# New durations, half clock and exclusion in a kernel's own list scheduler: two transformer blocks on one core

## The chip, the core and the metric

The kernel runs on one core of a Trainium2 chip. A core has five engines with a queue of instructions each: PE (TensorE, matmuls; its weight loads are listed as PEld), DVE (VectorE), ACT (ScalarE), POOL (GpSimd) and SP (SyncE, which here issues all DMAs). An engine takes its instructions strictly in the order of its queue and waits at each for semaphores of other engines. The metric is the device time of one execution in microseconds (us); lower is better. [...]

## The reference

Two blocks on x of shape (16, 512, 256), float32; every block has layer norm, a scale and shift per batch row, a token mixer, a gated residual, and the same again with a feed-forward part:

```python
h = _layernorm(x) * (1 + ca) + sa
x = x + ga * _L0_attn_ref(h, ...)      # fast weights: a recurrence over chunks of 16 tokens
h = _layernorm(x) * (1 + cb) + sb
x = x + gb * _L0_ffn_ref(h, ...)       # low rank, gelu
...
x = x + ga * _L1_attn_ref(h, ...)      # attention over a window of 64 tokens, 4 global tokens
x = x + gb * _L1_ffn_ref(h, ...)       # mix of a token with the one before, sigmoid * relu^2
```

The recurrence of the first block, per chunk and head, with two small weight matrices `W_in` and `W_out`:

```python
k_h = softmax(k_t . W_in) * lr;  q_h = softmax(q_t . W_in)
o_t = q_h . W_out + tril(q_h k_h^T) v_t
W_out = W_out + k_h^T v_t
for _ in range(2):
    g_out = -attn(W_in, k_t, v_t);  g_in = -attn(W_out, v_t, k_t)
    W_in = W_in - lr_in * g_in;     W_out = W_out - lr_out * g_out
```

## The kernel before

The work is cut into 16 units: 2 halves of the batch (8 rows each) times 8 blocks of 64 tokens. A unit `u` passes five streams:

- `prepare`: layer norm, projections to q, k, v (matmuls `pp`, L712), a short convolution on DVE (L731, three multiply-adds on `pp`), Silu on ACT, and spills of the results to DRAM (L740).
- `chain`: the recurrence. A unit has two pieces of 32 tokens, a piece two chunks of 16. `load_piece` brings a piece back (`dt_k`, `dt_v`, `dt_q`, L838) and scales it: ACT's square, DVE's reduction `ss_k`, `ss_q` (L850), Pool's product (L852). `recur` does a chunk. Its larger steps: scores of tokens and weights on DVE (L798 a product of 128x1024, L799 its sum), exponentials on ACT (L813), scalings on DVE (L820, L894), outer products on POOL (L805: `pd_o`, `pd_kv`, `pd_i`), their sums on DVE (L907). `pd_kv` is turned into running sums by an addition (L899), a scan (L902) and a copy (L903), all on DVE; POOL then makes the output of it (L932 to L934). `finish_piece` normalizes the output and stores it (L953).
- `mlp`: output projection (`pwo`, L979), residual, low-rank feed-forward (`ph`, `pQ`).
- `attend`: windowed attention. Per row group `r` of four: scores `sc` and their maxima (`mx`, L1160 on DVE, then with the global tokens' L1171, then copies on POOL, L486 and L488), scores again transposed (`st`), exponentials, `py` and `pz`, and the quotient `yT` on DVE (L1252, after `rs` on ACT, L1247 and L1248). The layer norm in front of it ends in `off_c` (L624), `xn_c` (L630), PE transposes and the scalings `hTc` (L638).
- `mix`: the second feed-forward part. `mixture` (L1301 on ACT, L1302 on DVE) blends a token with the one before.

The chains of the two halves run beside each other, and the streams of several units overlap: the program is written in the order of a coarse table of times (`timetable`). That order isn't the one that runs. When all instructions have been recorded, the class `Timetable` orders each engine's queue anew:

- `read` makes a `Step` of every instruction and finds from the tiles' cells which steps must come after which.
- `Step.cost` gives each step a duration: how long its engine is busy, and when its result is there.
- `run` is a list scheduler. Again and again it takes, over all engines, the step that can start first (ties: the first in program order), puts it at the end of its engine's queue, and marks when the engine is free and when the result is there. A step starts when its engine is free (`idle`), what it waits for has ended (`since`, with a `HOP` from engine to engine) and a buffer of its ring is free (`room`). On ACT, `table` keeps functions of another table in bursts.
- `pin` fixes the resulting order for every engine, and which tile follows which in a buffer.

So the durations set the order of all queues, PE's, DVE's, ACT's, POOL's and SP's, and nothing else of the program. Where DVE, ACT or POOL follow each other on the engine, the scheduler lets the next one start `EARLY` (83, 105 or 45 ns) before the result of the last.

## Time and profile before

| what | value |
|---|---|
| three runs | 3047.35, 3049.54, 3053.68 us (median 3049.54) |
| the profiled execution | 3055.67 us, of which 3053.9 us are the span from the first to the last instruction |
| mean granted clock of TensorE | 0.805 of full speed |
| DMA | 186.41 MB in 439304 packets, mean 61 GB/s |
| largest groups on POOL | L805 pd_i 303.6 us, pd_o 301.2, pd_kv 179.4; L932 156.3 |
| largest groups on DVE | L902 206.1 us, L1160 163.7, L798 sc_k 155.4, L907 di 154.2 |
| largest groups on PE | L1144 st 217.1 us, sc 201.9; L1274 pproj 129.0 |

A page of a profile gives the busy time of each engine, the span in 40 slices (each digit the busy share in tenths; PEclk the clock that TensorE was granted), the chain of work that ended last, and the costliest groups of instructions: line, engine, operation, result<-operands, count, then busy time and mean duration of one in ns, then the idle time of the engine in front of them and what ended it. A timeline row has start, duration, engine, line, operation. A matmul of float32 operands stands in the records as two.

### The profile page before, as it was taken

The numbers are of one execution on the slowest core, as the hardware profiler recorded it, in microseconds if no ns is written. First come the engines' busy times: TensorE is split into PE (matmuls) and PEld (weight loads), VectorE is DVE, ScalarE is ACT, GpSimd is POOL, SyncE is SP. The second block draws the span as 40 slices with busy tenths as digits, with TensorE's granted clock in tenths as the row PEclk, the third lists the DMA queues.
The fourth block names the chain that finished last, engine by engine and source line by source line (L and its number), as shares of the span: only waits on it lengthen the run. The fifth ranks groups of instructions, "written<-read, shape, count | busy, mean of one in ns | idle before, by whom it ended". The sixth has DMA issues, their size and how long they took to land.

```text
span 3053.9 us, 46422 instructions
## 1 busy us (share of the span) xinstructions
PE 2271.9 (74%) x16784; PEld 1407.7 (46%) x16784; DVE 2407.6 (79%) x4513; ACT 1705.7 (56%) x3805; POOL 1646.7 (54%) x1447
## 2 busy tenths in 40 slices
PE   3640156788878785887879788887978887898996
PEld 2210124454535354453545455463555555565664
DVE  1689889889898989879797988979697987975321
ACT  1771354575656565565656556575655645454553
POOL 0246656557565576656465565645556565654212
PEclk7775576888878796878879787888978787888998
DMA  5430113132305041230504123140413312122010
GB/s 158 100 68 7 49 35 75 36 81 53 88 22 119 21 102 39 61 80 22 117 24 105 36 68 73 35 106 22 116 25 75 67 53 60 39 63 60 22 29 28
DMA packets 439304, 186.41 MB, mean 61 GB/s; under 512 B 323937, under 2 KB 413090, under 8 KB 439074
## 3 DMA queue, kind: packets, MB, share of 16 engines
q1 hardware_dynamic: 439074, 183.44, 25.0%
q8 instruction: 132, 2.16, 0.3%
q14 instruction: 98, 0.80, 0.1%
HBM read 116.66 MB, written 66.72 MB: 60 GB/s over the span
## 4 chain that ended last, share of the span: by engine, by line
DVE 48%; PE 25%; ACT 11%; POOL 6%; issue 5%; DMA 3%; SPq 1%; POOLq 0%; DVEq 0%; ACTq 0%
DVE pd_kv L902 5%; PE st L1144 4%; DVE sc_v L798 4%; DVE sv L799 4%; DVE scs L799 3%; DVE sc_k L798 3%; DVE di L907 2%; DVE do L907 2%; DVE mx L1160 2%; DVE mix L1302 2%; PE pwo L979 2%; POOL pd_kv L805 2%; DVE pp L731 2%; PE sc L1144 2%; DVE sc_q L798 2%
## 5 line engine op out<-in xcount | busy, mean ns | idle before, releaser
L805 POOL TENSOR_TENSOR pd_o<-e_k,dt_v 128x1024 f32<-128x1024 f32 x128 | 301.2, 2361 | 273.6 <-DVE e_k L820 273.5
L805 POOL TENSOR_TENSOR pd_i<-e_v,dt_k 128x1024 f32<-128x1024 f32 x128 | 303.6, 2400 | 66.8 <-DVE e_v L820 66.8
L1144 PE MATMUL sc<-keys,qs 32*128 32x128 f32 x2048 | 201.9, 307 | 91.7 <-DVE yT L1252 61.1
L1144 PE MATMUL st<-qs,keys 32*128 32x128 f32 x2048 | 217.1, 339 | 68.5 <-DVE mx L1160 56.3
L1144 PEld LDWEIGHTS st<-qs,keys 32*128 32x128 f32 x2048 | 189.1, 233 | 108.1 <-DVE mx L1160 54.7
L1144 PEld LDWEIGHTS sc<-keys,qs 32*128 32x128 f32 x2048 | 164.9, 203 | 155.3 <-DVE yT L1252 65.7
L902 DVE TENSOR_TENSOR_SCAN pd_kv<-within,pd_kv 128x1024 f32<-128x1024 bf16 x64 | 206.1, 3220 | 0.7
L979 PE MATMUL pwo<-w_WoT,oT 128*128 128x256 f32 x256 | 95.9, 528 | 133.7 <-POOL oT L972 133.7
L932 POOL TENSOR_TENSOR pd_kv<-hid,pd_kv 128x1024 f32<-128x1024 f32 x64 | 156.3, 2442 | 60.3 <-DVE fw L903 58.9
L805 POOL TENSOR_TENSOR pd_kv<-hid,dt_v 128x1024 f32<-128x1024 f32 x64 | 179.4, 2803 | 17.0 <-DVE hid L894 17.0
L1160 DVE TENSOR_REDUCE mx<-sc 128x4 f32<-128x512 f32 x256 | 163.7, 676 | 26.1 <-PE sc L1141 25.7
L907 DVE TENSOR_REDUCE di<-pd_i 128x64 f32<-128x1024 f32 x128 | 154.2, 1210 | 29.5 <-POOL pd_i L805 29.4
L1196 ACT ACTIVATE pT<-st 128x512 f32<-128x512 f32 x256 | 133.5, 603 | 62.4 <-PE st L1141 62.4
L907 DVE TENSOR_REDUCE do<-pd_o 128x64 f32<-128x1024 f32 x126 | 151.8, 1205 | 12.3 <-POOL pd_o L805 12.1
L798 DVE TENSOR_TENSOR sc_k<-tok,fw 128x1024 f32<-128x1024 f32 x128 | 155.4, 1214 | 6.1 <-ACT tok L868 4.6
L798 DVE TENSOR_TENSOR sc_v<-tok,fw 128x1024 f32<-128x1024 f32 x128 | 151.4, 1216 | 1.8
L799 DVE TENSOR_REDUCE sv<-sc_v 128x64 f32<-128x1024 f32 x128 | 151.1, 1209 | 0.0
L1007 PE MATMUL ph<-PT,w_v 64*128 64x512 f32 x256 | 112.1, 800 | 39.6 <-ACT rs L1247 21.7
L1274 PE MATMUL pproj<-w_proj,yT 128*128 128x256 f32 x512 | 129.0, 404 | 15.2 <-ACT sg L495 8.3
L979 PEld LDWEIGHTS pwo<-w_WoT,oT 128*128 128x128 f32 x256 | 65.6, 273 | 150.5 <-POOL oT L972 135.7
L725 ACT COPY xp<-pp 128x512 f32<-128x512 f32 x96 | 56.9, 593 | 138.9 <-PE pp L712 131.7
L1252 DVE TENSOR_TENSOR yT<-py,rs 128x256 f32<-128x256 f32 x128 | 49.4, 415 | 104.3 <-ACT rs L1248 104.3
(244 smaller groups left out, 6605.4 us busy)
## 6 DMA issues: line engine op xcount, KB each, us to landing
values<-values SPq DMA_DIRECT2D x56, 256.0 KB
gate_a<-gates SPq DMA_DIRECT2D x64, 128.0 KB
xa<-in_x_dram SPq DMA_DIRECT2D x32, 256.0 KB
x<-in_x_dram SPq DMA_DIRECT2D x32, 256.0 KB
gate_c<-gates SPq DMA_DIRECT2D x64, 128.0 KB
gate_d<-gates SPq DMA_DIRECT2D x64, 128.0 KB
q<-y SPq DMA_DIRECT2D x64, 128.0 KB
dt_q<-q SPq DMA_DIRECT2D x32, 256.0 KB
```

Of the source, the lines that this page charges most:

```text
L798: engine.tensor_tensor(pr, tok.unsqueeze(1).to_broadcast(every), w.unsqueeze(2).to_broadcast(every), mul)
L799: nc.vector.tensor_reduce(dst, pr, AX.X, add)
L805: engine.tensor_tensor(pr, hid.unsqueeze(2).to_broadcast(every), tok.unsqueeze(1).to_broadcast(every), mul)
L902: nc.vector.tensor_tensor_scan(flat, within, flat, 0.0, mul, add)
L907: nc.vector.tensor_reduce(t, pr, AX.X, add)
L932: nc.gpsimd.tensor_tensor(po, qh.unsqueeze(2).to_broadcast([P, R, D, CH]), upto, mul)
L979: nc.tensor.matmul(po[:, n * C : (n + 1) * C], lhsT=pair(oT, k, 2 * b2 + n), rhs=w_o[:, k, :], start=k == 0, stop=k == 1,)
L1007: nc.tensor.matmul(ph, lhsT=w_v1[rows, f // 2, :], rhs=pT[rows], start=True, stop=True)
L1144: nc.tensor.matmul(dst, lhsT=lhsT, rhs=rhs, start=start, stop=False, skip_group_check=True)
L1160: nc.vector.tensor_reduce(mx[:, j], sc[j].rearrange("p (s k) -> p s k", s=NS), AX.X, ALU.max)
L1196: nc.scalar.activation(pT[j], st[j], AF.Exp)
L1274: nc.tensor.matmul(po[:, n * C : (n + 1) * C], lhsT=yT[:, k2, par].rearrange("p e t -> p (e t)"), rhs=w_proj[:, k2, par, :], start=k2 == 0 ...
```

## The change

The `Step` costs and the scheduler's loop change; all that computes stays. What is new:

```diff
-        self.busy, self.done = self.cost()
+        self.busy, self.rest = self.cost()
...
+        pair = [x for x in ins.ins if hasattr(x, "ap") and free(x) and x.bass_ap.space == bass.MemoryType.SB]
+        self.shares = len(pair) > 1
...
             if ins.is_transpose:
-                return 166, 273
+                return 2 * n / CLOCK, 165
             if str(w.dtype).endswith("bfloat16"):
-                return max(0.52 * n, 110), 0.52 * n + 115
-            rows, cols = list(w.ap)[0][1], size(w)
-            if min(rows, cols) <= 32 and n <= 256:
-                return (62, 275) if max(rows, cols) <= 32 else (0.38 * n + 55, 0.8 * n + 175)
-            return max(1.77 * n, 220), 1.75 * n + 150
+                own, wide = n / CLOCK, 1
+            else:
+                own, wide = max(4 * n / CLOCK, 140), P // max(32, list(w.ap)[0][1]) * (P // max(32, size(w)))
+            wide = min(wide, 4)
+            return own / wide, own - own / wide + (165 if wide == 1 else 65)
         if self.engine == "SP":
-            return 560, 3060
+            far = max(int(np.prod([n for _, n in list(x.ap)])) for x in aps)
+            return (600, LAND + 1300) if far > 2**16 else (530, LAND)
...
         elif self.kind == "InstTensorScalarPtr" and n == R * D * CH:
-            t = 190 + 2.1 * n
+            t = 2285
         else:
-            t = 150 + (1.65 if apart and self.kind == "InstTensorReduce" else 1.04) * n
-        return t - EARLY[self.engine], t
+            t = (150 if n > 64 else 165) + (1.65 if apart and self.kind == "InstTensorReduce" else 1.04) * n
+            t += 60 * (self.kind == "InstTensorScalarPtr")
+        return t - EARLY[self.engine], EARLY[self.engine]
...
                     t = max(t, idle[e], since[k])
+                    if e == "DVE" and steps[k].shares:
+                        t = max(t, pool)
+                    elif e == "Pool":
+                        t = max(t, lock)
...
-            idle[e] = t + s.busy + (TABLE if first else 0)
-            end[k] = t + s.done + (TABLE if first else 0)
+            busy = s.busy + (TABLE if first else 0)
+            if e == "PE":
+                while t >= edge:
+                    warm = used > (BUSY if warm else 0.97) * WINDOW
+                    edge, used = edge + WINDOW, 0.0
+                busy *= 1 if warm else 2
+                used += busy
+            idle[e] = t + busy
+            end[k] = t + busy + s.rest
+            if e == "Pool" and s.shares:
+                pool = end[k]
+            elif e == "DVE" and s.shares:
+                lock = end[k]
```

The constants are `CLOCK, WINDOW, BUSY = 2.4, 3413, 0.6` and `LAND = 2500`. All of the computation stands 22 lines further down in the changed kernel (L902 becomes L924).

More of the change, by code (lines that the diff above doesn't have):

```diff
@@ L104 @@
 TABLE = 1283
+CLOCK, WINDOW, BUSY = 2.4, 3413, 0.6
+LAND = 2500
 OTHER_TABLES = ("Silu", "Tanh", "Gelu_apprx_tanh")
@@ L130, in cost @@
             if ins.is_transpose:
-                return 166, 273
+                return 2 * n / CLOCK, 165
             if str(w.dtype).endswith("bfloat16"):
-                return max(0.52 * n, 110), 0.52 * n + 115
-            rows, cols = list(w.ap)[0][1], size(w)
-            if min(rows, cols) <= 32 and n <= 256:
-                return (62, 275) if max(rows, cols) <= 32 else (0.38 * n + 55, 0.8 * n + 175)
-            return max(1.77 * n, 220), 1.75 * n + 150
+                own, wide = n / CLOCK, 1
[3 more added lines that the diff above has]
+            return own / wide, own - own / wide + (165 if wide == 1 else 65)
         if self.engine == "SP":
-            return 560, 3060
+            far = max(int(np.prod([n for _, n in list(x.ap)])) for x in aps)
+            return (600, LAND + 1300) if far > 2**16 else (530, LAND)
         if self.kind == "InstLoadActFuncSet":
-            return TABLE, TABLE
+            return TABLE, 0
         if self.engine == "Activation":
@@ L280, in run @@
         self.owner, self.lines = {}, {e: [] for e in ENGINES}
-        held = None
+        held, pool, lock = None, 0.0, 0.0
+        warm, edge, used = False, WINDOW, 0.0
         def room(k):
```

## The prediction

> **What bounds the kernel now.** I read the page from the top, then one period of it in time.

> ```profile
> span 3053.9 us, 46422 instructions
> PE 2271.9 (74%) x16784; PEld 1407.7 (46%) x16784; DVE 2407.6 (79%) x4513; ACT 1705.7 (56%) x3805; POOL 1646.7 (54%) x1447
> DVE  1689889889898989879797988979697987975321
> PEclk7775576888878796878879787888978787888998
> DVE 48%; PE 25%; ACT 11%; POOL 6%; issue 5%; DMA 3%; SPq 1%; POOLq 0%; DVEq 0%; ACTq 0%
> ```

> DVE is busiest (79%) and holds 48% of the chain that ended last; PE holds 25%. In the slices DVE stands at 7 to 9 tenths but for the head and the last three slices, where PE has the work alone. The second view is the spread of three DVE operations with two SBUF tensors each: smallest, median and largest duration.

> ```profile
> L902 DVE TENSOR_TENSOR_SCAN pd_kv<-within,pd_kv x64: 2277/3220/4505, 137.0 to 2762.6; 128x1024 f32<-128x1024 bf16 x64
> L1302 DVE SCALAR_TENSOR_TENSOR mix<-hp,c_mu,mix x64: 700/752/2907, 673.7 to 3034.4; 128x512 f32<-128x512 f32 x64
> L1171 DVE TENSOR_TENSOR mx<-mx,mg x48: 165/187/2026, 1152.5 to 2990.2; 128x16 f32<-128x16 f32 x48
> ```

> One shape, and durations that differ by 2 us and more. The timeline says why:

> ```profile
> 1772.80 4.11 DVE L902 TENSOR_TENSOR_SCAN pd_kv<-within,pd_kv 128x1024 f32<-128x1024 bf16 x1
> 1772.42 2.34 POOL L805 TENSOR_TENSOR pd_o<-e_k,dt_v 128x1024 f32<-128x1024 f32 x1
> 1774.71 4.35 POOL L805 TENSOR_TENSOR pd_kv<-hid,dt_v 128x1024 f32<-128x1024 f32 x1
> ```

> The scan waits until Pool's pd_o is through (1774.76) and then runs its 2.2 us, to 1776.91; Pool's next product was issued at 1774.71 and stands still in its turn, 4.35 us instead of 2.34. So the two exclude each other, and a DVE operation that waits goes ahead of Pool's next one. What is lost so on DVE: scans 206.1 us busy less 64 x 2.277 = 60; mix 64 x 1.424 (the group's mean) less 64 x 0.752 = 43; mx 48 x 0.676 less 48 x 0.187 = 23. Together 126 us, 4% of the span.

> From 362 to 2572 us the scans come in groups of four, one unit of work each, 13 intervals of 146 to 180 us; five intervals in the middle are 175 us to within 0.5 and repeat each other. One of them in slices (columns: length, then busy time of PE, PE's loads, DVE, ACT, POOL, granted clock, DMA), its DVE waits, and three rows of the DMA queue:

> ```profile
> 1772.80:1797.80 25.00, 23.24 (x78) 11.88 (x77) 23.77 (x34) 12.77 (x24) 20.74 (x13) 0.87 0.06 18
> 1822.80:1847.80 25.00, 25.00 (x198) 15.36 (x196) 12.21 (x25) 21.07 (x50) 8.01 (x9) 0.85 0.46 110
> 1872.80:1897.80 25.00, 19.97 (x209) 14.72 (x209) 24.01 (x47) 15.01 (x35) 21.64 (x18) 0.62 0.27 54
> ...
> DVE pp L731 <- ACT pp L728: 8.4, 2, 7.9
> DVE ss_q L850 <- ACT sq_q L829: 5.9, 1, 5.9
> DVE yT L1252 <- ACT rs L1248: 4.3, 3, 3.6
> ...
> 1841.16 1.71 SPq L953 DMA_DIRECT2D o<-dt_q  x2
> 1845.03 2.40 SPq L740 DMA_DIRECT2D k<-y  x4
> 1847.48 1.12 SPq L838 DMA_DIRECT2D dt_q<-q  x2
> ```

> Most of a period belongs to DVE, but one stretch belongs to PE: there PE is busy 25.00 of 25 us, DVE 12.21. DVE's waits in a period come to some 24 us, 19 of them in and just behind that stretch. Exclusion costs it another 9.5 us (two scans 1.8 and 1.7, two mix 1.5 and 2.1, two mx 1.3 and 1.1). A period is thus about 140 us of DVE work, 10 of exclusion and 24 of waiting.

> **The change part by part.** No instruction is added, removed or resized. The hand-written scheduler gets other durations, a model of PE's half clock and of the exclusion, and so each engine's queue has another order. I set the queues of the two built programs beside each other (line numbers of before). DVE work is summed with the median durations of the trace.

> *Mix (L1302).* Before, the first pair of a unit stands straight behind the e_v scaling (L820) that lets Pool start its last two of four pd_i (10.11 us in one run at 1904.78), and stalls there twice, 1.5 and 2.1 us. After, it stands behind the third pd_i's reduction (1.2 us) and a score reduction (1.2 us), that is 2.4 us after the third pd_i ended, when the fourth, 2.34 us long, is just through; Pool's next is a cast that waits for a later DVE step. Of the 43 us I take 38 away. Bounds: 43 if all dodge, 0 if DVE comes a little early. Mix is 7 us of work later; behind it wait pka's matmuls and ACT's Relu, whose Pool square keeps its place in Pool's queue, so that I charge nothing; without this slack it is 7 us in each of 13 periods.

> *mx (L1171).* Some move behind a reduction, some only onto the next Pool product. Of 23 us, 6 are taken; bounds 20 and -10.

> *Scans (L902).* Before, 0.27 us of work stand between the addition L899 and the scan; in 1 of 64 it is 2 us or more. After it is 2.2 us on average, in 29 of 64 2 us or more; in a steady period 2.8, 0.2, 1.2 and 8.6. This is less than it seems. The scan of the first half has two Pool products behind its own, pd_o and the other half's pd_kv, ending 2.34 and 4.68 us later. A scan issued 3.1 us later (0.26 + 2.8) has missed the first boundary and waits 1.6 us for the second; before, it waited 1.8 us for the first. The scheduler has Pool's next instruction ready 45 ns before the last one's end and so always sends Pool first, which the chip did not do above. I take 0; bounds -25 and +25 (half of the 60 either way is more than the rows allow).

> *PE's stretch.* The new prices fit the rows better: two 512-column matmuls are 1.71 us apart from the next two (pq at 1842.86, pk at 1844.57), 0.855 each, against 0.853 now and 0.906 before; sixteen 32-column ones took 1.08 us in all, against 0.85 now and 1.66 before. In the queues the reductions mx of a window's last row group (L1160) move forward by 23 us of DVE work (from 83.0 to 60.2 after a period's first scan), off_c (L624), which PE's transposes wait for, by 3 us, and ACT's second rs moves ahead of the hTc scalings, which is what yT waited 3.6 us for. But pp's matmul of the key weights stays behind the same scores and masks. I take 2 of the 13 us off yT's and pp's waits, 13 times: 26. Bounds 0 and 75 (half of the longest of each, 3.6 and 7.9, 13 times).

> *The DMA queue and the second half.* The store of the second o (L953) moves behind the first two spills k<-y (L740). Before, both stores were issued by 1842.9 and the first spill at 1845.03, at 0.6 each; so this store comes some 3.9 us later, and behind it the load dt_q, ACT's square, DVE's ss_q, which is waited for already. ss_q itself also moves behind two mx reductions (1.3 us). I charge 1.5 us in each of 13 periods, 20 in all; bounds 0 and 51. The second half's pd_i reduction is 8.3 us of work later in the period. The load dt_k behind it was issued at 1808.3 and its square ran at 1841, 33 us on, so that I charge nothing; without that slack it is 13 x 8.3 = 108.

> [...] The row is the granted clock, 0.805 over the span: 39% of the time at half speed, and 0.62 to 0.87 in the slices above. [...]

> Sum: -38 - 6 + 0 - 26 + 20 = -50. The profiled execution took 3055.67 us (span 3053.9 and 1.8 around it), 6 above the median of the runs, 3049.54. So 3055.7 - 50 = 3006, and 3000 on the scale of the median.

> **The rivals.** *Holes close.* With the last row group's maxima 23 us earlier, half of yT's and pp's waits goes (75) beside the exclusions (44), and the later store is hidden: 3049.5 - 119 = 2930. For it: PE is busy only 12 to 20 of 25 us elsewhere in a period. Against it: PE's queue around pp has nearly the same order. *Nothing comes of it.* Stalls before Pool turn into waits for Pool: in place of the early scan DVE waits for the reduction of pd_o, 0.9 us. 3050, within 15. *Slower: the recurrence sets the period.* The scan of the second half is put off by 8.6 us of other DVE work, where the chip would have let it through after one Pool product. If the two halves' chain, not DVE's work, ends a period, its 8.3 us count whole: 13 x 8.3 = 108, less 44 saved: 3049.5 + 64 = 3113. Against it: the 33 us of slack behind dt_k; for it: 19 us of idle DVE, part of which waits for the q chain. It decides once ss_q's wait grows beyond what the pp wait gives up. That the change doesn't do what it says is no rival: the orders differ.

> **How the numbers follow.** Forecast 0.46 (2965 to 3035), holes close 0.16, nothing 0.16, slower 0.22. Runs of this kernel spread by 0.2%, about what can be told from no change. Faster: 0.44 + 0.16 + 0.05 = 0.65; within 0.2%: 0.02 + 0.06 = 0.08; slower 0.05 + 0.22 = 0.27. The range 2925 to 3100 holds the forecast, "nothing", about two thirds of the first rival and under half of the last; 2965 to 3035 is the forecast's own.

> **What would show it.** Mix's mean falls from 1424 ns to below 900; the scan's mean stays above 2.9 us; the period of the scans shrinks from 175 to about 171 us; in PE's stretch DVE's wait for pp shrinks by 1 to 3 us, that for ss_q grows by 1 to 4. I am wrong if the scans' mean drops to 2.4 us (the exclusion is then planned away), if the wait for ss_q grows by 8 us (the chain sets the end), or if mix keeps its 1424 ns.

## The result, and the profile after

The changed kernel takes 3083.15 us (median; 3080.13 to 3088.16), the kernel before, run beside it, 3048.44: ratio 1.0121, 95% interval 1.0088 to 1.0154. It is slower, by 1.2%. The profiled execution took 3081.6 us. All lines of code stand 22 further down than before (the scan L902 is L924). The page, in the rows shown of before:

```profile
span 3079.8 us, 46411 instructions
...
PE 2278.5 (74%) x16784; PEld 1407.7 (46%) x16784; DVE 2294.7 (75%) x4513; ACT 1704.0 (55%) x3805; POOL 1622.8 (53%) x1447
...
DVE  1689898777878978887796978878796878874221
...
PEclk7775576878879796888879788878879886879988
...
DVE 39%; PE 36%; ACT 10%; POOL 7%; issue 4%; DMA 3%; SPq 1%; POOLq 0%; DVEq 0%; ACTq 0%
```

DVE has 113 us less to do (2407.6 to 2294.7) and the span is 26 us longer. So DVE stands idle for 785.1 us (span less busy time) where it was 646.3: 139 more. In the chain that ended last DVE's share fell from 48 to 39%, and PE's rose from 25 to 36%. The three DVE operations with two SBUF tensors each (SBUF is the memory in which all of Pool's operands lie too), smallest, median and largest ns:

```profile
L924 DVE TENSOR_TENSOR_SCAN pd_kv<-within,pd_kv x64: 2262/2279/3305, 138.9 to 2777.5; 128x1024 f32<-128x1024 bf16 x64
L1324 DVE SCALAR_TENSOR_TENSOR mix<-hp,c_mu,mix x64: 698/743/1679, 700.5 to 3060.4; 128x512 f32<-128x512 f32 x64
L1193 DVE TENSOR_TENSOR mx<-mx,mg x48: 149/178/1159, 1159.1 to 3015.6; 128x16 f32<-128x16 f32 x48
```

Most of the exclusion has in fact been planned away. The scan's median is now its undisturbed time (2279 ns, where the shortest scan before took 2277); means fell from 3220 to 2481 ns (scan), 1424 to 771 (mix) and 676 to 395 (mx): 47, 42 and 13 us. What came in its place stands in DVE's waits (total, times, longest, in us):

```profile
DVE mx L1182 <- PE sc L1163: 146.7, 46, 14.7
DVE yT L1274 <- ACT rs L1270: 73.0, 18, 11.2
DVE pp L753 <- ACT pp L750: 50.5, 38, 5.0
...
DVE ss_q L872 <- ACT sq_q L851: 34.3, 9, 9.9
...
DVE up_b L680 <- PE pv L1052: 28.2, 18, 14.8
...
DVE mg L1190 <- PE sg L1166: 23.1, 9, 13.4
```

Before, the first two of these were

```profile
DVE yT L1252 <- ACT rs L1248: 104.3, 33, 12.0
...
DVE mx L1160 <- PE sc L1141: 25.7, 14, 6.2
```

and pp stood at 58.5, ss_q at 52.2, up_b at 14.9, mg at 5.9. Summed over all rows of this view by the engine that ended the wait, DVE's idle time for PE rose from 104.0 to 249.6 us; for ACT it fell from 376.0 to 354.9, for Pool it went from 70.5 to 83.8. That is the whole account: 113 us less work, 146 more waiting for TensorE, and small change. The steady interval between units went from 175.2 to 173.6 us (mean of four, from the first scan of the tenth unit on). So the 26 us aren't lost in the steady units. Up to that scan the program is 16 us later than before (1613.9 against 1597.6), the four intervals are 6.5 us shorter together (694.3 against 700.8), and 16 us are lost behind them, 11 of these after the last scan (291.3 to 302.3). DVE's idle time for PE rose in all three parts: from 34 to 96, from 2 to 28 and from 68 to 126 us. In the steady units the gain and the new waits nearly cancel; where the streams start and run out the waits win.

In three slices of a steady unit (columns as before), the middle one again PE's, DVE is now idle at the unit's start too:

```profile
1786.60:1811.60 25.00, 24.86 (x140) 14.45 (x141) 17.75 (x24) 12.47 (x22) 8.61 (x8) 1.00 0.10 23
1836.60:1861.60 25.00, 25.00 (x196) 14.38 (x195) 12.49 (x28) 23.89 (x56) 9.23 (x9) 0.94 0.49 121
1886.60:1911.60 25.00, 16.93 (x187) 13.30 (x191) 24.34 (x50) 12.97 (x31) 24.05 (x22) 0.64 0.28 54
```

The timeline in the first of them, PE's rows and then DVE's (start, duration, then what it is; in brackets the idle time before it):

```profile
1788.83 0.60 PE L1353 MATMUL pr<-w_W_rT,mix 128*128 128x256 f32 x2
1789.36 1.08 PE L1036 MATMUL pQ<-z,w_U 128*64 128x512 f32 x4
1790.36 0.70 PE L1353 MATMUL pr<-w_W_rT,mix 128*128 128x256 f32 x2
1790.99 1.07 PE L1036 MATMUL pQ<-z,w_U 128*64 128x512 f32 x2
1792.00 1.13 PE L1353 MATMUL pr<-w_W_rT,mix 128*128 128x256 f32 x4
1793.06 1.07 PE L1036 MATMUL pQ<-z,w_U 128*64 128x512 f32 x2
1794.06 1.17 PE L1166 MATMUL sc<-keys,qs 32*128 32x128 f32 x32
1795.16 1.04 PE L1163 MATMUL sc<-masks,ident_bf 128*128 128x512 bf16 x4
...
1789.99 0.25 DVE L925 COPY fw<-pd_kv 128x64 f32<-128x64 f32 x1
1795.59 1.89 DVE L1182 TENSOR_REDUCE mx<-sc 128x4 f32<-128x512 f32 x3 [5.36 <-PE sc L1163]
```

DVE's next instruction in its queue is a reduction of scores, and PE, busy without a gap, has yet to come to them: 5.36 us of idle DVE. DVE keeps to its queue meanwhile: all 4513 of its instructions start in this trace in the order in which the program has them. The planner's own times for these steps have no idle time at this place. From the first ph of this unit to the last mask matmul they allow 14.4 us; on the chip it was 21.05 (1775.15 to 1796.20), of which 2.2 us are waits of ph for ACT and DVE (the plan has 1.8 us of waits there). One pQ matmul (two records) is priced at 0.43 us at full clock since its 64 columns are taken to run beside another's; the chip needed 1.01 for one alone (1790.99 to 1792.00) and 1.00 for two in a row (1789.36 to 1790.36), at a granted clock of 1.00 in this slice. So in these rows two took no longer than one, and the new price gives the discount also to one that stands alone. Over the run the planner has PE busy for 1907 us, the chip 2278; before, it was 2030 and 2272. So the plan was short before too, by 242 us, and is now by 371.

Not all of it is PE's price: of the 146.7 us of this wait the plan itself contains 50 (before, 28 beside the chip's 25.7), with 6.8, 8.6 and 11.9 in front of three reductions that on the chip waited 11.4, 10.9 and 14.7.

### The profile page after: what moved, and what is told of

It is laid out like the page before. It is cut to its first block, busy times and chain, and to the rows that moved or that the text cites. A ratio compares the mean times of both kernels' runs of the same rounds, so it can differ in the third digit from the quotient of the medians.

```text
span 3079.8 us, 46411 instructions
## 1 busy us (share of the span) xinstructions
PE 2278.5 (74%) x16784; PEld 1407.7 (46%) x16784; DVE 2294.7 (75%) x4513; ACT 1704.0 (55%) x3805; POOL 1622.8 (53%) x1447
## 4 chain that ended last, share of the span: by engine, by line
DVE 39%; PE 36%; ACT 10%; POOL 7%; issue 4%; DMA 3%; SPq 1%; POOLq 0%; DVEq 0%; ACTq 0%
DVE sc_k L820 4%; DVE scs L821 4%; PE pQ L1036 3%; DVE sv L821 3%; PE st L1166 3%; DVE sc_v L820 3%; PE pproj L1296 3%; DVE pd_kv L924 3%; PE sc L1166 3%; DVE di L929 3%; PE ph L1029 2%; PE pr L1353 2%; PE pp L734 2%; DVE do L929 2%; POOL pd_o L827 2%
## 5 line engine op out<-in xcount | busy, mean ns | idle before, releaser
L827 POOL TENSOR_TENSOR pd_i<-e_v,dt_k 128x1024 f32<-128x1024 f32 x128 | 296.0, 2348 | 75.4 <-DVE e_v L842 71.4
L1166 PE MATMUL st<-qs,keys 32*128 32x128 f32 x2048 | 237.4, 340 | 109.8 <-DVE mx L1182 43.6
L1182 DVE TENSOR_REDUCE mx<-sc 128x4 f32<-128x512 f32 x256 | 165.1, 679 | 146.7 <-PE sc L1163 146.7
L1166 PEld LDWEIGHTS st<-qs,keys 32*128 32x128 f32 x2048 | 206.3, 233 | 144.9 <-DVE mx L1182 51.6
L1166 PE MATMUL sc<-keys,qs 32*128 32x128 f32 x2048 | 195.5, 301 | 40.6 <-DVE mx L1182 31.2
L1166 PEld LDWEIGHTS sc<-keys,qs 32*128 32x128 f32 x2048 | 161.2, 200 | 110.3 <-issue 42.0
L954 POOL TENSOR_TENSOR pd_kv<-hid,pd_kv 128x1024 f32<-128x1024 f32 x64 | 170.5, 2668 | 56.0 <-DVE fw L925 51.3
L1218 ACT ACTIVATE pT<-st 128x512 f32<-128x512 f32 x256 | 133.0, 602 | 62.5 <-PE st L1163 61.5
L820 DVE TENSOR_TENSOR sc_k<-tok,fw 128x1024 f32<-128x1024 f32 x128 | 155.4, 1214 | 4.7 <-ACT tok L890 3.0
L924 DVE TENSOR_TENSOR_SCAN pd_kv<-within,pd_kv 128x1024 f32<-128x1024 bf16 x64 | 158.4, 2481 | 0.3
L820 DVE TENSOR_TENSOR sc_v<-tok,fw 128x1024 f32<-128x1024 f32 x128 | 153.0, 1215 | 4.4 <-POOL dt_q L956 2.6
L827 POOL TENSOR_TENSOR pd_kv<-hid,dt_v 128x1024 f32<-128x1024 f32 x64 | 151.8, 2372 | 3.9 <-DVE hid L916 3.9
L508 POOL CAST maxima<-mx 128x16 bf16<-128x16 f32 x64 | 34.4, 538 | 208.6 <-DVE mx L1193 94.5
L654 PE MATMUL pt_a<-blocks,xn_a 128*128 128x128 f32 x128 | 32.8, 374 | 133.2 <-ACT xn_a L652 130.0
L1296 PE MATMUL pproj<-w_proj,yT 128*128 128x256 f32 x512 | 122.2, 385 | 6.0 <-DVE yT L1274 5.1
```

The source lines that it names most:

```text
L820: engine.tensor_tensor(pr, tok.unsqueeze(1).to_broadcast(every), w.unsqueeze(2).to_broadcast(every), mul)
L827: engine.tensor_tensor(pr, hid.unsqueeze(2).to_broadcast(every), tok.unsqueeze(1).to_broadcast(every), mul)
L924: nc.vector.tensor_tensor_scan(flat, within, flat, 0.0, mul, add)
L954: nc.gpsimd.tensor_tensor(po, qh.unsqueeze(2).to_broadcast([P, R, D, CH]), upto, mul)
L1166: nc.tensor.matmul(dst, lhsT=lhsT, rhs=rhs, start=start, stop=False, skip_group_check=True)
L1182: nc.vector.tensor_reduce(mx[:, j], sc[j].rearrange("p (s k) -> p s k", s=NS), AX.X, ALU.max)
```

## The experiments

Each experiment edits only the planner; what is computed stays. Five theories are numbered in the expectations: (1) TensorE is planned too fast, (2) the exclusion in the plan costs, (3) the clock's windows spoil the order, (4) it is the chance of near ties, (5) the rule of who goes next costs, in any setting. Busy time, idle time and scans are of the profiled execution. "Idle" columns are DVE's, from the waits view: all rows ended by PE, all ended by Pool, and the row of mx for sc. The ratio is to the kernel before, run on the same chip beside it.

| kernel | us | ratio, 95% interval | DVE busy | idle for PE | for Pool | mx for sc | scan mean ns |
|---|---|---|---|---|---|---|---|
| before | 3048.44 | | 2407.6 | 104.0 | 70.5 | 25.7 | 3220 |
| the change | 3083.15 | 1.0121 [1.0088, 1.0154] | 2294.7 | 249.6 | 83.8 | 146.7 | 2481 |
| e1 old PE prices | 3019.44 | 0.9899 [0.9867, 0.9930] | 2296.4 | 150.0 | 112.6 | 51.4 | 2536 |
| e2 no exclusion | 3047.08 | 0.9985 [0.9963, 1.0007] | 2395.3 | 169.7 | 62.5 | 94.9 | 2976 |
| e3 exclusion alone | 3022.24 | 0.9905 [0.9874, 0.9936] | 2294.0 | 133.8 | 111.5 | 52.9 | 2558 |
| e4 PE prices and clock alone | 3082.85 | 1.0123 [1.0076, 1.0170] | 2415.7 | 172.7 | 44.1 | 92.4 | 3071 |
| e5 change, PE never slowed | 3103.54 | 1.0149 [1.0129, 1.0168] | 2296.2 | 300.0 | 74.5 | 140.5 | 2451 |
| e6 change, PE x 1.25 | 3005.59 | 0.9833 [0.9804, 0.9863] | 2304.7 | 161.6 | 96.2 | 89.0 | 2453 |
| e7 change, PE x 1.02 | 3043.42 | 0.9971 [0.9944, 0.9999] | 2292.9 | 226.8 | 87.2 | 126.9 | 2502 |
| e8 before, PE x 1.02 | 3050.01 | 0.9991 [0.9969, 1.0013] | 2413.8 | 113.0 | 73.4 | 33.4 | 3124 |
| e9 change, mx 3 us later | 3075.97 | 1.0075 [1.0045, 1.0104] | 2296.6 | 193.7 | 92.8 | 24.0 | 2503 |
| e10 = e1, DVE first | 2940.93 | 0.9631 [0.9601, 0.9660] | 2340.1 | 131.5 | 44.5 | 47.0 | 2863 |
| e11 change, PE x 0.98 | 3067.96 | 1.0060 [1.0040, 1.0081] | 2298.2 | 262.5 | 86.5 | 161.2 | 2482 |
| e12 change, PE x 1.45 | 3006.44 | 0.9848 [0.9817, 0.9878] | 2298.8 | 98.4 | 106.9 | 41.4 | 2463 |
| e13 change, DVE first | 3017.23 | 0.9892 [0.9858, 0.9926] | 2365.1 | 203.9 | 41.6 | 111.7 | 2634 |
| e14 = e6, DVE first | 3037.08 | 0.9955 [0.9933, 0.9978] | 2383.7 | 138.1 | 51.2 | 72.1 | 2733 |
| e15 = e10, PE x 1.02 | 2993.76 | 0.9821 [0.9793, 0.9848] | 2354.5 | 130.4 | 42.9 | 51.7 | 2833 |
| e16 DVE and queue terms alone | 3037.27 | 0.9953 [0.9932, 0.9973] | 2398.5 | 123.3 | 52.6 | 29.2 | 3124 |
| e17 = e10, PE x 0.98 | 2975.18 | 0.9765 [0.9738, 0.9792] | 2340.7 | 155.1 | 48.4 | 49.2 | 2812 |
| e18 = e1, PE x 1.02 | 3016.13 | 0.9901 [0.9868, 0.9935] | 2300.3 | 159.1 | 109.4 | 52.9 | 2578 |

**The parts apart: e1 to e4, e16.** In e1 the five lines of PE prices are those of before and the clock's doubling is gone; e3 has only the exclusion; e4 only PE's prices and clock; e2 and e16 leave the exclusion out. e3 and e4 also have VectorE's and the queue's durations of before.

```diff
 e1, e3, e16
-                busy *= 1 if warm else 2
 e2, e4, e16
-                    if e == "DVE" and steps[k].shares:
-                        t = max(t, pool)
-                    elif e == "Pool":
-                        t = max(t, lock)
```

> The changed kernel with TensorE's old prices and without the clock model: the exclusion, VectorE's and the queue's new durations stay. Theory 1 (TensorE priced too low moves the mx reductions ahead of their scores, and VectorE's queue waits there): the wait of L1182 for sc falls from 146.7 us to under 50, the scans stay at 2.5 us, and the time falls to about 2990 us (2960 to 3020). Theory 2 (the exclusion in the model is what costs, by steps held back until GpSimd is done): the time stays at 3080 us or rises, with the wait gone or not.

> The changed kernel without the exclusion in the planner (the two lines that hold a step behind the other engine's); TensorE's, VectorE's and the queue's new durations stay. Theory 1: the scans are stalled again (mean above 3.0 us, some 100 us in all) and the wait for sc stays above 60 us, so the time rises to about 3150 us (3110 to 3190). Theory 2: the time falls to about 3010 us.

> The kernel before with the exclusion alone added: all its old durations stay. Theory 1: scans fall to 2.5 us and the wait for sc stays small, time about 2990 us (2950 to 3020). Theory 2: about 3080 us or more, since the exclusion alone does the harm.

> The kernel before with TensorE's new prices and clock alone: no exclusion, VectorE's and the queue's old durations. Theory 1: the wait for sc comes up as in the changed kernel (above 60 us) while the scans stay stalled, time about 3150 us (3100 to 3190). Theory 2: 3000 to 3050 us, no slower than before.

> The kernel before with only VectorE's and the queue's new durations: no exclusion, TensorE's old prices, no clock. If these small terms matter by themselves (they seemed to bring 36 us beside TensorE's new prices): 3020 us or less. If that was spread of the order: 3035 to 3065 us.

Alone, the exclusion brings 1% and PE's prices cost 1.2%. With the exclusion, old PE prices give 3019 and 3022, new ones 3083. Theory 2 fell: the exclusion alone does no harm. Theory 1 got the sign of e1, e3 and e4 right but the sizes too large: the gains are 30 us, not 60 (e1 lies at the edge of its range, its wait for sc at 51.4 us just above what was expected, e3 2 us outside its range), and e4 is 3083, not 3150 (its wait for sc, 92 us, came). e2 (3047) missed theory 1 by 100 us and theory 2 by 37. Beside PE's new prices the exclusion seemed to cost 36 us, and e2 and e4, which differ only in DVE's and the queue's durations, lie 36 us apart too. That made the spread of the order itself a suspect. e16, 3037 with these small terms only, lies where it was expected if they bring nothing but spread: some 15 us come and go with them, and no run shows why.

In e1 DVE's waits show what the exclusion costs in return (compare 12.1, 29.4 and 17.1 before for these rows of Pool's; the one that grew is pd_o's):

```profile
DVE mx L1181 <- PE sc L1162: 51.4, 19, 7.1
DVE do L928 <- POOL pd_o L826: 45.2, 28, 2.0
...
DVE di L928 <- POOL pd_i L826: 27.6, 14, 3.2
...
DVE pd_kv L920 <- POOL pd_kv L826: 18.8, 25, 1.9
```

**How fast TensorE is planned: e5 to e8, e11, e12.** One factor:

```diff
 e5
-                busy *= 1 if warm else 2
 e6 (e7: 1.02 and 2.04; e11: 0.98 and 1.96; e12: 1.45 and 2.9)
-                busy *= 1 if warm else 2
+                busy *= 1.25 if warm else 2.5
```

> The changed kernel with TensorE never slowed in the planner (the doubling of the clock model taken out): its plan now has TensorE busy for 1568 us instead of 1907, where the chip shows 2278. Theory 1 (TensorE planned too fast, scores planned too early): the mx reductions move still further ahead, the wait for sc rises above 170 us, and the time to about 3120 us (3090 to 3150). Theory 3 (the clock's windows, not the prices, spoil the order: the same row is priced differently from window to window): the wait falls below 90 us and the time to about 3030 us.

> The changed kernel with every TensorE duration in the planner, at either clock, 1.25 times as long: TensorE's plan is then busy for 2186 us, near the chip's 2278. Theory 1: the wait for sc falls to under 80 us and the time to about 3025 us (3005 to 3045), near that of the old prices with the exclusion (3019 us). Theory 3: the windows are still there, so the wait stays above 110 us and the time at 3070 us or more.

> The changed kernel with every TensorE duration in the planner 1.45 times as long: TensorE's plan is busy for 2388 us, 5% over the chip's 2278. Theory 1: the wait for sc falls below 60 us; the time stays in the range of the 1.25 (2990 to 3025 us), since steps planned too late cost as little as the old prices did. Theory 4: a draw between 3000 and 3100 us with no bond to the wait.

> The changed kernel with every TensorE duration in the planner 2% longer: a change too small to mean anything by itself, to see how far the time moves when only ties and near ties in the order fall differently. Theory 1: the wait for sc stays between 120 and 160 us and the time within 12 us of the changed kernel's (3071 to 3095). Theory 4 (the order is so sensitive that any nudge moves the time by 1%, and the change's loss is one such draw): more than 20 us off, on either side.

> The changed kernel with every TensorE duration in the planner 2% shorter. With 2% longer it took 3043 us, so a second draw. Theory 1 with a spread of the order on top: the wait for sc 120 to 160 us, time 3040 to 3090 us, so that the mean of the three is slower than or equal to before. Theory 4 (no trend, spread alone): anywhere from 3000 to 3100 us.

> The kernel before with every TensorE duration in the planner 2% longer. Theory 1: 3040 to 3065 us, scans stalled as before (mean 3.1 to 3.3 us). Theory 4: more than 20 us off 3052 us on either side.

From the fastest planned TensorE to the slowest the times are 3104, 3068, 3083, 3043, 3006 and 3006 us, and DVE's idle time for PE 300, 263, 250, 227, 162 and 98. With e1, e3 and e18 there are five kernels with this exclusion and a slower-planned TensorE (busy for 2034 us in the plan of e1, 2186 in e6, 2388 in e12), 3006 to 3022 us; the four with the new prices, prices within 2% of them, or faster ones lie at 3043 to 3104. So the size of TensorE's durations is what costs, and not the clock's windows: e6 and e12 have windows too and are fast. The trend is shown, the single step isn't: 2% either way moved the changed kernel by 15 and 40 us; the kernel before stayed within 4. With 2% more the loss against before is gone (0.9971). The three draws (kernels that differ only by such a nudge) 3068, 3083 and 3043 average 3065, so of the 35 us lost some 15 are what draws of this kind lose on average, by these three, and some 20 are how near ties fell in this one; with three draws this is an estimate. Of what was expected, e8 and e12 came as theory 1 had it. e5's time did, but its wait for sc is 140.5 us where it was to rise above 170: the added idle time for PE stands in other rows. e6 did but for a wait of 89 us in place of under 80, and e11 but for one of 161 in place of at most 160. e7 fell on theory 4's side, and theory 4 keeps its part.

**Is it the place of the reductions? e9.** 

```diff
+                if e == "PE" and to == "DVE" and steps[j].ins.outs[0].bass_ap.tensor.name.startswith("mx"):
+                    since[j] = max(since[j], end[k] + 3000)
```

> The changed kernel, with one hop lengthened in the planner: a mx reduction (L1182) may be placed 3 us after its scores at the earliest, where it was 55 ns; no price is touched. Theory 1 (the reductions stand ahead of scores that are late on the chip): the wait for sc falls from 146.7 us to under 50 and the time to about 3025 us (3000 to 3045). If the waits only show what TensorE does anyway, the wait moves to other rows and the time stays at 3065 us or more.

The wait for sc went as foretold, the time didn't: 3076. The idle time turned up in other rows:

```profile
DVE yT L1276 <- ACT rs L1272: 98.5, 24, 16.1
...
DVE up_b L682 <- PE pv L1054: 56.6, 27, 14.8
DVE mg L1192 <- PE sg L1168: 55.2, 22, 8.5
...
DVE mx L1184 <- PE sc L1165: 24.0, 18, 3.2
```

So the reduction that waits is where the loss shows, and not what makes it. PE as a whole comes later than the plan has it, and whatever DVE step stands next then waits. Theory 1 holds only in its wider form.

**Who goes next at Pool's boundary: e10, e13, e14, e15, e17, e18.** In the change a Pool product is free to be followed 45 ns before its result is there (EARLY), and a DVE step waits for the result; so, of two that wait, Pool always wins in the plan. One line turns that:

```diff
             if e == "Pool" and s.shares:
-                pool = end[k]
+                pool = idle[e] - 1
```

> The old TensorE prices with the exclusion (first experiment, 3019 us), with one rule of the exclusion turned: when GpSimd has operations back to back, a VectorE step that waits gets the next turn in the plan, as the chip gave it to the scan (a scan that waited for pd_o until 1774.76 us ran ahead of the pd_kv that GpSimd had issued). In the plan GpSimd's next operation always won, since its queue is free 45 ns before its result is there. If that costs: steady period from 170.9 to about 166 us and the time about 2985 us (2960 to 3005). If not: 3010 to 3030 us, with GpSimd's operations stalled in exchange.

> The changed kernel with one line turned: in the planner's exclusion a waiting VectorE step goes before GpSimd's next operation. TensorE's new prices and clock stay. Theory 5 (the rule of who goes next costs some 80 us in any setting, TensorE's prices some 60 more): 3000 us (2980 to 3025), so faster than before, with the wait for sc still above 90 us. Theory 1 alone (TensorE's prices decide, the rule helps only where they are right): 3060 us or more.

> The changed kernel with the rule turned and every TensorE duration 1.25 times as long in the planner. Theory 5: both gains add, 2930 us (2910 to 2955), the wait for sc under 90 us. If the two mend the same loss: 2985 to 3010 us, as with the 1.25 alone.

> The fast version (old TensorE prices, exclusion, rule turned: 2941 us) with every TensorE duration 2% longer in the planner. Theory 5: 2925 to 2965 us. Theory 4 (a lucky draw): back at 3000 us or more.

> The fast version (old TensorE prices, exclusion, rule turned: 2941 us, with 2% longer TensorE 2994) with every TensorE duration 2% shorter in the planner. Theory 5: 2935 to 3000 us, so that all three lie below the version with GpSimd first. Theory 4: 3005 us or more.

> The first experiment (old TensorE prices, exclusion as in the change: 3019 us) with every TensorE duration 2% longer in the planner. Theory 5 (and theory 1, for which these prices are the right ones): 3005 to 3035 us. Theory 4: below 2995 us or above 3045.

On the old PE prices three draws with DVE first take 2941, 2975 and 2994 us, three with Pool first 3016, 3019 and 3022 (e3 among them): 49 us on average, no overlap. e10 went further than expected (2941 us where 2960 to 3005 was, a steady interval of 160 to 162 us where 166 was); e17 and e18 came as theory 5 had it. On the change itself the line turns 1.0121 into 0.9892 (e13, as expected). So the loss against before goes by either of two edits, slower PE prices or this rule. On PE x 1.25 it cost 31 us (3006 to 3037), against the expectation, and mix stalls there again (its median is 1662 ns, 744 in e6); so theory 5 doesn't hold in any setting, and why is open. e15, too, missed what was expected of it, by 29 us. The fastest, e10, beats both kernels at 0.9631 [0.9601, 0.9660]; with its neighbours at 0.9765 and 0.9821, about 1% of it is a good draw. The timeline of e1, one unit's first scan:

```profile
1784.16 0.26 DVE L920 TENSOR_TENSOR pd_kv<-pd_kv,fw 128x64 f32<-128x64 f32 x1 [0.63 <-POOL pd_kv L826]
1786.45 1.22 DVE L928 TENSOR_REDUCE do<-pd_o 128x64 f32<-128x1024 f32 x1 [2.03 <-POOL pd_o L826]
1787.59 3.28 DVE L923 TENSOR_TENSOR_SCAN pd_kv<-within,pd_kv 128x1024 f32<-128x1024 bf16 x1
```

The scan's input is there at 1784.42, DVE then idles 2.03 us for pd_o and the scan ends at 1790.87. In e10, with Pool's products beside it:

```profile
1728.22 2.34 POOL L826 TENSOR_TENSOR pd_o<-e_k,dt_v 128x1024 f32<-128x1024 f32 x1
1730.52 4.33 POOL L826 TENSOR_TENSOR pd_kv<-hid,dt_v 128x1024 f32<-128x1024 f32 x1
...
1728.30 0.26 DVE L920 TENSOR_TENSOR pd_kv<-pd_kv,fw 128x64 f32<-128x64 f32 x1 [0.61 <-POOL pd_kv L826]
1728.60 4.11 DVE L923 TENSOR_TENSOR_SCAN pd_kv<-within,pd_kv 128x1024 f32<-128x1024 bf16 x1
1732.63 1.19 DVE L928 TENSOR_REDUCE do<-pd_o 128x64 f32<-128x1024 f32 x1
```

Here the scan is issued at once, stalls 1.83 us for pd_o, and is through 4.15 us after its input (1728.56 to 1732.71), where it was 6.45; the stalled one is Pool's pd_kv (4.33), and pd_o's reduction finds its operand there. In numbers over the run: DVE's busy time rises by 44 us (stalls among it), its idle time for Pool falls by 68, for ACT by 30, for PE by 19.

## Why the prediction was wrong

*Mix, -38.* Right: 1424 to 771 ns is 42 us, within the bounds.

*mx, -6.* Too small: 13 us, within the bounds.

*Scans, 0.* Wrong, outside its ±25: 47 us were saved. The step said that "a scan issued 3.1 us later (0.26 + 2.8) has missed the first boundary and waits 1.6 us for the second". That set the new place of the scan against Pool's old times. The plan had put the scan behind Pool's whole run of products, and the chip followed: in the steady period shown three of the four scans took 2277 to 2279 ns, and one 3276. The sign "the scan's mean stays above 2.9 us" failed (2481). The gain was in DVE's busy time alone; part of its price is DVE's wait for Pool's run of products, which e10 takes away (DVE's idle time for Pool is 112.6 us in e1 and 44.5 in e10).

*PE's stretch, -26.* This is the step that turned the sign. What it credited came: yT's and pp's waits fell by 31 and 8 us. But it took "the reductions mx of a window's last row group (L1160) move forward by 23 us of DVE work" for a gain and didn't ask whether their scores move forward too. In the plan the reductions stand directly behind their scores, at times that PE doesn't keep. The row "DVE mx <- PE sc" rose by 121 us and all of DVE's waits for PE by 146. The prediction had seen the new prices "fit the rows better" from two full-size matmuls and from sixteen 32-column ones, although for the second the new price was too short already (0.85 us for 1.08); pQ and ph, which were then planned too short, weren't held against a row, though the trace had them. The wait that replaces a stall must be looked for on the engine whose price was cut. That the row itself isn't the cause (e9) doesn't save the step: the sum put PE coming later than planned at nothing, and the runs show 146 us more of idle DVE there, which falls from 250 to 162 and 98 us, and the loss with it, when PE is planned 1.25 and 1.45 times as slow (e6, e12).

*The queue, +20.* The wait for ss_q fell from 52.2 to 34.3 us; no sign of the late store in it, and in the steady unit shown above ss_q doesn't wait at all (5.9 before), where the prediction's sign was 1 to 4 us more. Its sign for pp came (8.4 to 6.7 us in that unit).

*The clock.* The sum has no term for the clock model. The granted clock over the span hardly moved, 0.805 before and 0.804 after. Taking the model out cost 20 us (3083.15 to 3103.54, e5), but this also planned PE still faster, so that its worth by itself wasn't measured.

*The sum* had DVE's work fall by 44 us, where it fell by 113, and its idle time by 6 (26 less 20), where it rose by 139. Of the rivals, the slower one had the right side and the wrong mechanism: no 8 us came into ss_q's wait, and the steady interval shrank by 1.6 us (to 171 was the sign). The time, 3083, lies in the range, but on the wrong side of before.

*What stays open.* How much of the 35 us is this draw of near ties (e7 and e11 put it near 20); which of PE's new prices costs most (pricing pQ and ph without the discount, and nothing else, wasn't tried); why e13's rule alone also undoes the loss; and why turning the boundary's rule costs at PE x 1.25. To the second, the plan's times can be set against the trace, from the start of one matmul to the start of the next: the plan is short by 129 us on sc, 51 on st, 43 on pQ and 13 on ph. Before, it was short by 87 on sc and 10 on st, and 14 and 9 too long on pQ and ph. So pQ's shortfall rose most, but the scores' is the largest.

## What to carry to other kernels

A planner's durations must not be cut on one engine without holding their sum against the chip: prices that are too short (1907 us planned, 2278 run) send the others' in-order queues ahead to wait, and a 100 us gain elsewhere is eaten. They needn't be exact: with the exclusion, plans of 2034 us (e1) and of 2388 (e12), one under and one over the 2278 that PE is busy in the changed kernel, were both faster than before (0.9899 and 0.9848). When an engine's busy time falls and the span doesn't, add up that engine's idle time by the engine that ended it, and don't repair the row that shows the wait before the one that makes it. Nudge a list scheduler's durations by 2% before believing a 1% result: here it moved the time by 3 to 53 us.

## What was not expected of the hardware

The stalls of the exclusion cost less here than the order that avoids them: e10 has the scans at 2863 ns and takes 2940.93 us, e1 with 2536 ns takes 3019.44. In the rows of e10 the one that was issued first went first: the scan, issued at 1728.60 in pd_o's time, ran before pd_kv, which Pool issued at 1730.52. A plan that lets Pool's back-to-back product in first is not what the chip did in these rows.

The granted clock of the profiled executions went with the time: 0.80 to 0.81 in the kernels above 3030 us, 0.813 to 0.823 in those of 2941 to 3022. That is a bond, not a shown cause.
